# Third layer of a position-bias network on tiles of 32 keys, by a third level of lane sums carried out by DMA

## The chip, the cores and the metric

The kernel runs on one core of a Trainium2 chip. The metric is device time in microseconds (us), lower is better; a time is one execution of the whole program. All data are float32.

## What is computed

Two layers in a row on an input of 2 × 512 × 32 × 32. The first is deformable attention with eight heads followed by a two-layer perceptron; the second is a plain attention over the 1024 positions. The change lies in the first one's position bias, which costs most: for every batch and head (16 groups), every query (1024) and every sampled key (64), a small network 2 → 128 → 128 → 1 is applied to the distance between them.

```python
pos = grid_q[:, :, None, :] - grid_kv[:, None, :, :]
bias = jnp.sign(pos) * jnp.log1p(jnp.abs(pos))
bias = jax.nn.relu(bias @ cpb_w1 + cpb_b1)
bias = jax.nn.relu(bias @ cpb_w2 + cpb_b2)
bias = (bias @ cpb_w3 + cpb_b3).reshape(b, GROUPS, H * W, Hd * Wd)
sim = jnp.einsum('bhid,bhjd->bhij', qh, kh) + bias
attn = jax.nn.softmax(sim, axis=-1)
out = jnp.einsum('bhij,bhjd->bhid', attn, vh)
```

`pos` has two coordinates, so the first layer's value for a query (y, x) and a key is a sum of one table entry for x and one for y, then a relu.

## The kernel before

**The main loop.** There are 16 groups of 16 slots (`NS` = 256 steps in all); a slot is four keys of one group against all 1024 queries. A group is one head of one batch: a block of 128 channels holds two heads. Step s of the loop (L847 on) does the following.

- `st_layer1(s + 2)` (L681): VectorE (DVE) makes the first layer's 128 channels × 4096 values of a slot, two steps ahead, from tables `ta` and `tb`. The tables come from a DMA into `fb` (L650, on SP's queue), once in four steps.
- `st_layer2(s)` (L698): TensorE (PE) multiplies by the second layer's weights. The 128 output channels are taken in four quarters z; each quarter fills a PSUM tile `ps` of two banks in which the four keys lie in four blocks of 32 partitions, and is made of eight float32 matmuls, each of which shows as two instructions. ScalarE (ACT) evicts each quarter with bias and relu: z = 0 and 2 to `rx` (L707), z = 1 and 3 to the sums and to `ub` (L709). There are three `ps` tiles.
- `st_sum(s, z)` (L717): DVE adds two quarters. With z = 2 GpSimd (POOL) then issues an accumulating DMA that adds `ub` to the slot's sum tile (L719).

After that a slot's sum tile holds, for each of four keys, 32 partial sums (lanes) over 1024 queries. The second layer's channels were ordered beforehand (`rank`, `order`, `arrange`), so that the third layer is a sum with signs over lanes.

**The lane sums.** The third layer on PE (`st_layer3`, L784) takes a tile of 128 partitions whatever is in it, so the tiles are first made denser by DMAs from SBUF to SBUF. `st_fold(s)` adds the odd lanes of a tile to the even ones; the odd lanes are free then, and `st_join(s)` puts the next slot's sum in them: a copy on SP's queue (L743) and an accumulating DMA on POOL's (L736). The tile then holds eight keys of 16 lanes. `st_fold2` and `st_join2` do the same once more with pairs of lanes (copy L752), which gives 16 keys of eight lanes. Each of them takes two DMAs[...]. `added[0]` is the newest lane sum; `add` issues each sum behind it on POOL with `tc.issue_after`, which orders issue on one engine and waits for nothing.

**The order in the loop.** A pair of slots that begins at a has its fold in step a + 2 and its join (copy and sum) in step a + 3. Four slots from a have `st_fold2` in step a + 4 and `st_join2` in step a + 6. Every eight slots `st_layer3` runs twelve steps after their first: four matmuls, one for each half of the queries and each of two tiles of 16 keys, in four column blocks of 32. Two such calls fill the group's `sim`, to which the query-key products (`QUADS`, L767) are added. The steps of the softmax (`softmax_steps`) are spread over the following steps behind an eviction. The last slots go to the third layer without the sums (weights `w3u`).

**Buffers.** The sum tiles are `ua` (four buffers, every fourth slot), `uc` (two, every fourth slot), `uo` (three, every second slot); `ub` and `rx` have three each. A sum tile is written by ACT in its own step and is free when its last reader is through: for `uc` and `uo` a join's DMA, for `ua` the third layer.

**Background.** Queries, offsets, sampled keys and values are made in small portions between the steps (`chain`, `sample`), in five chains. `prod` holds 12 tap products of the offset convolution; its borders are cleared once, in `arrange`. After the loop come the output projection (`project`), the perceptron and the second layer.

Of the kernel before, what the change touches and what calls it, by code (L numbers as in the profile page):

```python
# [57 lines left out]
def conv_seq_kernel(ctx: ExitStack, tc: tile.TileContext, x, xt, kst, pst, cst, vec, wsm, outw, w1, w2, wl, wlt, brow, out):  # L58
# [25 lines left out]
    w3f = cp.tile([P, 48], F32, name="w3f")  # L84
# [122 lines left out]
    with tc.tile_pool(name="lp", bufs=2) as lp:  # L207
# [11 lines left out]
        prod = ph.tile([P, 12, 2, 8, 8], F32, name="prod")  # L219
# [22 lines left out]
        nc.gpsimd.dma_start(out=pz[:, 0:413], in_=pst)  # L242
        nc.gpsimd.dma_start(out=ident, in_=kst)

        def load(b, k, wq=None):
# [21 lines left out]
        w2t, crow, tri, eight, chan, mask = (  # L267
            pz[:, a:b] for a, b in ((0, 128), (128, 256), (256, 384), (384, 392), (392, 393), (393, 413))
        )
        wb = vs[:, VOFF["w3"] : VOFF["w3"] + 2]  # L270
        po_, rn, t8, pc, dc, k8, one = (
            pw_[:, a:b] for a, b in ((0, 1), (1, 3), (3, 4), (4, 5), (5, 6), (8, 16), (128, 256))
# [15 lines left out]
        def order():  # L288
            nc.vector.tensor_scalar(k8, eight, rn[:, 1:2], 8.0, ALU.is_le, ALU.mult)
            nc.vector.tensor_reduce(t8, k8, AX.X, ALU.add)  # L290
# [6 lines left out]
        def arrange():  # L297
            nc.gpsimd.memset(prod, 0.0)
# [17 lines left out]
            nc.gpsimd.tensor_scalar(w3f[:, 16:32], mask[:, 0:16], sc[:, 8:9], None, ALU.mult)  # L316
            nc.gpsimd.tensor_scalar(w3u[:, 28:32], mask[:, 16:20], sc[:, 8:9], None, ALU.mult)
# [4 lines left out]
        def chain(ci):  # L322
# [52 lines left out]
            else:  # L375


                for m in range(3):
# [71 lines left out]
            fe = ph.tile([P, 5, n], F32, tag="fe", name="fe")  # L450
            pos, ab, u, ln, er = (fe[0:64, i, :] for i in range(5))
            nc.vector.tensor_scalar(pos, thf[0:64, 2 * n : 3 * n], -1.0, gq[0:64], ALU.mult, ALU.add)
# [8 lines left out]
            nc.vector.scalar_tensor_tensor(er, u, 1.0, ab, ALU.subtract, ALU.subtract)  # L461
            rc = acc.rearrange("p a k y x -> p (a k y x)")[0:64, 0:n]
            nc.vector.reciprocal(rc, u)
            nc.vector.tensor_tensor(er, er, rc, ALU.mult)
            nc.vector.tensor_scalar(pos, pos, 0.0, 2.0, ALU.is_ge, ALU.mult)
            yield
            nc.vector.tensor_tensor(ln, ln, er, ALU.subtract)
# [10 lines left out]
        def sample(ci):  # L478
# [10 lines left out]
            sg = ph.tile([P, 5, 2, K * J], F32, tag="fe", name="sg")  # L489
            hat = sg[:, 0:4].rearrange("p a f j -> p (a f j)")[:, 0 : 4 * K * J]  # L490
# [4 lines left out]
            nc.vector.tensor_tensor(sg[:, 4], sg[:, 0], sg[:, 1], ALU.mult)  # L495
            hx = ph.tile([P, 2, K, J], F32, tag="hx", name="hx")
# [5 lines left out]
            for i, (b, k) in enumerate(G):  # L502
                g = b * NCH + k
                xnt = ph.tile([P, 8, P], F32, name="xnt")
# [12 lines left out]
                kv, uv = (ph.tile([P, J], F32, name=name) for name in ("kv", "uv"))  # L517
                rowwise, natural = "p (e i t) -> p e i t", "p (i e t) -> p e i t"
                for f in range(2):
                    r, v = slice(64 * f, 64 * f + 64), sg[:, 4, f, i * J : (i + 1) * J]  # L520
                    nc.scalar.activation(
                        uv[r].rearrange(rowwise, e=2, t=16), v[r].rearrange(natural, e=2, t=16), AF.Copy,
                        scale=col("bn1b", k)[r],
                    )
# [6 lines left out]
                for t in range(8):  # L531
# [5 lines left out]
                nc.scalar.activation(  # L537
                    kv.rearrange(rowwise, e=2, t=16), ps[:, 0:J].rearrange(natural, e=2, t=16), AF.Copy,
                    scale=bns[:, k : k + 1],
                )  # L540
# [150 lines left out]
        def st_layer2(s):  # L691
            h1 = h1s.pop(s)
            r = []
            for z in range(4):
                ps = zp.tile([P, 2, 512], F32, name="ps2")
                for h in range(2):
# [6 lines left out]
                    ("rx", 3), (("ua", 4), ("uo", 3), ("uc", 2), ("uo", 3))[s % 4], ("rx", 3), ("ub", 3)  # L703
# [34 lines left out]

        def st_fold(s):
            add(lanes(s, 0), lanes(s, 1))  # L740

        def st_join(s):
            nc.sync.dma_start(out=lanes(s, 1), in_=lanes(s + 1, 1))  # L743
            add(lanes(s, 1), lanes(s + 1, 0))
# [4 lines left out]

        def st_join2(s):  # L750
            for o, i in zip(twos(s, 1), twos(s + 2, 1)):
                nc.sync.dma_start(out=o, in_=i)  # L752
            for o, i in zip(twos(s, 1), twos(s + 2, 0)):
                add(o, i)


        def st_layer3(s):
            gi, i = divmod(s // 8, NSL // 8)
            b, k, f = groups[gi]
            if gi not in sims:  # L760
                sims[gi] = simp.tile([P, 512], F32, name="sim")
            if f == 0 and i == 1:

                assert state[chain_of[b, k][0]] is None
                sims[gi + 1] = simp.tile([P, 512], F32, name="sim")
                for f_, h_, o, h in QUADS:
                    nc.tensor.matmul(  # L767
                        sims[gi + o][h_, :], kz[f_, b * NCH + k, :], qa[f_, b, k, h * 512 : (h + 1) * 512],
                        start=(o == 1), stop=False,
                    )  # L770
            w = w3f[:, 16 - 16 * i : 48 - 16 * i]
            parts = [[(w, sums[s + 4 * e][1])] for e in range(2)]
            if s + 8 == NS:

                w = [w3u[:, 28 - 16 * i - 4 * o : 60 - 16 * i - 4 * o] for o in range(4)]
                parts[1] = [(w[o], sums[s + 4 + o][1]) for o in range(4)]
                parts[1].append((w[3], sums[s + 7][3]))
                parts[0] = 4 * [None] + parts[0]
            for m in range(len(parts[1])):
                for h in range(2):  # L780
                    for e in range(2):
                        if parts[e][m]:
                            q, (w_, t) = 64 * h + 32 * e, parts[e][m]
                            nc.tensor.matmul(  # L784
                                sims[gi][q : q + 32, :], w_, t[:, h, :], start=(i == 0 and f == 0),
                                stop=(i == 1 and m == len(parts[e]) - 1),
                            )
# [762 lines left out]
```

## Time and profile before

| What | us |
|---|---|
| median of 3 runs | 2618.96 |
| lowest and highest run | 2618.88, 2620.72 |
| profiled execution, time | 2621.32 |
| profiled execution, span of the core | 2619.2 |
| of it: start of the main loop's matmuls | 37.6 |
| of it: after the loop, from the first matmul of the projection | 1895.6 to 2619.2 |

A busy time is the time in which an engine executes instructions, summed without overlap. PEld is the load of weights into PE, beside the matmuls. In a row of instructions, `out<-in` names the tiles; then come shapes, count, busy time, mean duration in ns, and the idle time of the engine just before these instructions with what ended it.

The DMA queues, their packets, bytes and the share of the 16 DMA engines' time:

```profile
q0 software_dynamic: 100736, 259.43, 54.6%
q1 hardware_dynamic: 66144, 144.93, 15.8%
```

q0 is POOL's queue (the accumulating DMAs), q1 that of SP and ACT.

### The profile page before, as it was taken

The numbers are of one execution on the slowest core, as the hardware profiler recorded it, in microseconds if no ns is written. First come the engines' busy times: TensorE is split into PE (matmuls) and PEld (weight loads), VectorE is DVE, ScalarE is ACT, GpSimd is POOL, SyncE is SP. The second block draws the span as 40 slices with busy tenths as digits, with TensorE's granted clock in tenths as the row PEclk, the third lists the DMA queues.
The fourth block names the chain that finished last, engine by engine and source line by source line (L and its number), as shares of the span: only waits on it lengthen the run. The fifth ranks groups of instructions, "written<-read, shape, count | busy, mean of one in ns | idle before, by whom it ended". The sixth has DMA issues, their size and how long they took to land.

```text
span 2619.2 us, 48156 instructions
## 1 busy us (share of the span) xinstructions
PE 2603.2 (99%) x19752; PEld 1019.5 (39%) x19752; DVE 2313.1 (88%) x1463; ACT 1750.3 (67%) x2325; POOL 815.7 (31%) x909
## 2 busy tenths in 40 slices
PE   9999999999999999999999999999999999999999
PEld 3333322333233232333333333334355665646556
DVE  7999999999999999999999999999776587666656
ACT  5887898878888887887887777777733242314041
POOL 1333333333333333333333333333332334200100
PEclk9999999999999999999999999999999999999999
DMA  5788877888887888787887888788787768400202
GB/s 188 176 174 185 190 171 168 182 182 195 169 178 171 180 171 200 173 179 166 185 182 165 180 177 177 167 185 177 151 211 169 150 143 172 91 17 1 73 0 57
DMA packets 167531, 407.74 MB, mean 156 GB/s; under 512 B 24944, under 2 KB 73216, under 8 KB 164624
## 3 DMA queue, kind: packets, MB, share of 16 engines
q0 software_dynamic: 100736, 259.43, 54.6%
q1 hardware_dynamic: 66144, 144.93, 15.8%
q8 instruction: 156, 2.56, 0.4%
q14 instruction: 63, 0.52, 0.1%
q10 hardware_dynamic: 432, 0.31, 0.0%
HBM read 82.15 MB, written 6.55 MB: 34 GB/s over the span
## 4 chain that ended last, share of the span: by engine, by line
PE 93%; DVE 3%; ACT 2%; issue 1%; DMA 0%; DVEq 0%; ACTq 0%
PE ps L698 64%; PE sw L1041 7%; PE sw L1200 7%; PE sw L160 6%; PE sw L988 2%; PE sw L1298 2%; PE sim L784 1%; PE psg L600 1%; DVE hm L137 1%; ACT rx L707 1%; PE psx L1276 1%; PE pkv L534 0%; PE sim L767 0%; PE pt L801 0%; PE pb L834 0%
## 5 line engine op out<-in xcount | busy, mean ns | idle before, releaser
L698 PE MATMUL ps<-h,cw 128*32 128x512 f32 x16384 | 1776.0, 592 | 6.1 <-ACT rx L707 5.0
L681 DVE CUSTOM_DVE_ANT_1 h<-ta,tb 128x4096 f32<-128x4096 f32 (+1 forms) x257 | 1130.5, 4399 | 29.6 <-PE ps L698 26.8
L698 PEld LDWEIGHTS ps<-h,cw 128*32 128x32 f32 x16384 | 538.0, 110 | 1209.1 <-issue 1144.6
L707 ACT ACTIVATE rx<-ps,sc 128x1024 f32<-128x1024 f32 x512 | 568.2, 1110 | 146.3 <-PE ps L698 125.7
L709 ACT ACTIVATE ub<-ps,sc 128x1024 f32<-128x1024 f32 x256 | 308.3, 1204 | 92.7 <-PE ps L698 92.6
L717 DVE SCALAR_TENSOR_TENSOR ub<-rx,sc,ub 128x1024 f32<-128x1024 f32 x256 | 326.3, 1275 | 6.6 <-ACT ub L709 6.6
L736 POOL DMA_DIRECT2D ua<-uc x126 | 154.8, 1241 | 301.6 <-DMA ua<-uc 291.7
L736 POOL DMA_DIRECT2D ua<-ua x189 | 219.0, 1319 | 28.8 <-DMA ua<-uo 22.3
L719 POOL DMA_DIRECT2D uo<-ub x127 | 124.4, 980 | 232.3 <-DVE ub L717 217.6
L1041 PE MATMUL sw<-hm,w2t 128*128 128x512 f32 x448 | 193.8, 592 | 0.2 <-DVE hm L125 0.2
L709 ACT ACTIVATE uo<-ps,sc 128x1024 f32<-128x1024 f32 x128 | 154.3, 1205 | 51.4 <-PE ps L698 51.0
L717 DVE SCALAR_TENSOR_TENSOR uo<-rx,sc,uo 128x1024 f32<-128x1024 f32 x128 | 163.3, 1276 | 8.1 <-ACT uo L709 8.1
L736 POOL DMA_DIRECT2D uc<-uo x63 | 53.1, 842 | 319.4 <-DMA uc<-uo 314.4
L1041 PEld LDWEIGHTS sw<-hm,w2t 128*128 128x128 f32 x448 | 85.0, 190 | 104.3 <-issue 99.0
L137 DVE TENSOR_TENSOR hm<-hm,sw 128x512 f32<-128x512 f32 (+1 forms) x80 | 58.7, 738 | 70.4 <-PE sw L160 50.6
L719 POOL DMA_DIRECT2D ua<-ub x64 | 58.9, 921 | 170.8 <-DVE ub L717 163.5
L661 ACT ACTIVATE ta<-fb,vs 128x512 f32<-128x512 f32 (+1 forms) x65 | 89.3, 1377 | 8.0 <-DMA fb<-fdr 8.0
L709 ACT ACTIVATE ua<-ps,sc 128x1024 f32<-128x1024 f32 x64 | 77.1, 1204 | 20.4 <-PE ps L698 20.1
L709 ACT ACTIVATE uc<-ps,sc 128x1024 f32<-128x1024 f32 x64 | 77.2, 1206 | 20.2 <-PE ps L698 17.1
L1364 POOL DMA_DIRECT2D xs<-rs x6 | 7.2, 1195 | 259.2 <-DVE rs L137 259.2
L166 ACT COPY hm<-sw 128x512 f32<-128x512 f32 x24 | 14.1, 586 | 110.1 <-PE sw L160 110.1
L717 DVE SCALAR_TENSOR_TENSOR uc<-rx,sc,uc 128x1024 f32<-128x1024 f32 x64 | 81.6, 1275 | 2.7 <-ACT uc L709 2.5
(294 smaller groups left out, 2657.7 us busy)
## 6 DMA issues: line engine op xcount, KB each, us to landing
uo<-ub POOLq DMA_DIRECT2D x127, 512.0 KB, 5.5
fb<-fdr SPq DMA_DIRECT2D x64, 512.0 KB, 5.2
ua<-ub POOLq DMA_DIRECT2D x64, 512.0 KB, 5.7
uc<-ub POOLq DMA_DIRECT2D x64, 512.0 KB, 5.1
ua<-ua POOLq DMA_DIRECT2D x63, 256.0 KB, 6.2
ua<-uo SPq DMA_DIRECT2D x63, 256.0 KB, 2.4
ua<-uo POOLq DMA_DIRECT2D x63, 256.0 KB, 5.8
uc<-uc POOLq DMA_DIRECT2D x63, 256.0 KB, 6.9
```

What stands on the lines that cost most here:

```text
L137: nc.vector.tensor_tensor(out, a, b_, op)
L160: nc.tensor.matmul(bank[:, e, :], w, x, start=(q in (1, 2, 5) and e == k == 0), stop=True, skip_group_check=True,)
L661: nc.scalar.activation(ta.rearrange("p j x -> p x j")[:, :, j0:j1], fb[:, 0, :, j0:j1], AF.Identity, bias=col("cb1"), scale=col("w1x"),)
L681: nc.vector._custom_dve(TENSOR_ADD_SAT, out=h1[:, y : y + step].rearrange("p y t x -> p (y t x)"), in0=a.unsqueeze(1).to_broadcast([P, ste ...
L698: nc.tensor.matmul(ps[32 * q : 32 * q + 32, h, :], cw2[:, 32 * z : 32 * z + 32], h1[:, 16 * h : 16 * h + 16, q, :], start=True, stop=True,)
L707: nc.scalar.activation(o, ps, AF.Relu, bias=sc[:, 4 + z : 5 + z])
L709: nc.scalar.activation(o, ps, AF.Relu, bias=sc[:, 4 + z : 5 + z], scale=sc[:, z : z + 1])
L717: nc.vector.scalar_tensor_tensor(r[1], r[0], sc[:, z : z + 1], r[1], ALU.mult, ALU.add)
L719: nc.gpsimd.dma_start(out=sums[s][1], in_=sums[s][3], accum_op=ALU.add)
L736: nc.gpsimd.dma_start(out=out, in_=in_, accum_op=ALU.add)
L1041: nc.tensor.matmul(ps[:, m, :], w[:, a, k, m * P : (m + 1) * P], x[:, b_, k, :], start=(k == 0), stop=(k == 1),)
L1200: nc.tensor.matmul(ps[:, m, :], w[:, a, k, c + m * P : c + (m + 1) * P], x[b_][:, k, :], start=(k == 0), stop=(k == nk - 1),)
```

## The change

**A third level of lane sums.** `fours`, `st_fold3`, `st_copy3` and `st_join3` treat eight slots as the second level treats four: partitions of a tile are taken as 16 blocks of two times four, and each of fold, copy and join takes four DMAs of 16 partitions × 1024 elements (64 KB). A tile then holds 32 keys of four lanes. This is done for slots below `FULL` (208), which are groups 0 to 12; groups 13 to 15 stay with 16 keys to a tile.

**The third layer.** `st_layer3` takes a whole group: in groups 0 to 12 four matmuls on two tiles, in groups 13 and 14 eight on four tiles, in group 15 sixteen at the end as before, of which four stood in a call of their own. The query-key products open both of the `sim` tiles of a pair. The call stands 27 steps after the group's first slot (22 in groups 13 and 14), and the softmax steps are queued from there. Before, the second call of a group stood 20 steps after its first slot.

**The order.** A table `LEVELS` names the steps: fold, copy and join of the first level 2, 3 and 4 steps after a pair's first slot, of the second 6, 7 and 8 steps after, of the third 11, 14 and 15. The joins' copies are now moves of their own one step ahead of the sums, issued through `move`, which puts the SP copy into `tc.issue_after(added[0])`. In the last group times are near those of before (`LAST`).

**Buffers.** `ua` becomes `u8` (four buffers, every eighth slot) and `u4` (two, every eighth slot, four slots later). To make room `prod` shares the gather's buffer `xnt` and is cleared on POOL in each of chains 1 to 4, `fe` and `sg` shrink from five parts to three by working in place, `hx` shares `acc`, `kv` and `uv` share `gof`, and `opt` is allocated after the loop. The keys stay in natural order, so `uv` and `kv` are plain copies.

**Constants.** `order` needs one comparison in place of a comparison and a sum; the weight masks `w3f` are wider.

```diff
-                    ("rx", 3), (("ua", 4), ("uo", 3), ("uc", 2), ("uo", 3))[s % 4], ("rx", 3), ("ub", 3)
+                    ("rx", 3), (("u8", 4), ("uo", 3), ("uc", 2), ("uo", 3), ("u4", 2), ("uo", 3), ("uc", 2), ("uo", 3))[s % 8],
+                    ("rx", 3), ("ub", 3),
...
+        def move(out, in_):
+            with tc.issue_after(added[0]):
+                nc.sync.dma_start(out=out, in_=in_)
+
         def st_fold(s):
             add(lanes(s, 0), lanes(s, 1))
 
+        def st_copy(s):
+            move(lanes(s, 1), lanes(s + 1, 1))
+
         def st_join(s):
-            nc.sync.dma_start(out=lanes(s, 1), in_=lanes(s + 1, 1))
             add(lanes(s, 1), lanes(s + 1, 0))
...
+        def st_copy2(s):
+            for o, i in zip(twos(s, 1), twos(s + 2, 1)):
+                move(o, i)
+
         def st_join2(s):
-            for o, i in zip(twos(s, 1), twos(s + 2, 1)):
-                nc.sync.dma_start(out=o, in_=i)
             for o, i in zip(twos(s, 1), twos(s + 2, 0)):
                 add(o, i)
 
+        def fours(s, i):
+            t = sums[s][1].rearrange("(l a e) h n -> l a e (h n)", a=2, e=4)[:, i]
+            return [t[:, e] for e in range(4)]
+
+        def st_fold3(s):
+            for o, i in zip(fours(s, 0), fours(s, 1)):
+                add(o, i)
+
+        def st_copy3(s):
+            for o, i in zip(fours(s, 1), fours(s + 4, 1)):
+                move(o, i)
+
+        def st_join3(s):
+            for o, i in zip(fours(s, 1), fours(s + 4, 0)):
+                add(o, i)
+
+        FULL = NS - 3 * NSL
+        LEVELS = (
+            (8, FULL, (st_copy3, st_join3, st_fold3), (14, 15, 11)),
+            (4, NS - 4, (st_copy2, st_join2, st_fold2), (7, 8, 6)),
+            (2, NS - 4, (st_copy, st_join, st_fold), (3, 4, 2)),
+        )
+        LAST = {st_copy2: 6, st_join2: 6, st_fold2: 4, st_join: 3}
+        due = {}
+        for step, end, moves, times in LEVELS:
+            for kind in range(3):
+                for a in range(0, end, step):
+                    t = times[kind] if a < NS - NSL else LAST.get(moves[kind], times[kind])
+                    due.setdefault(a + t, []).append((kind > 0, moves[kind], a))
...
         def st_layer3(s):
-            gi, i = divmod(s // 8, NSL // 8)
+            gi = s // NSL
...
-            w = w3f[:, 16 - 16 * i : 48 - 16 * i]
-            parts = [[(w, sums[s + 4 * e][1])] for e in range(2)]
-            if s + 8 == NS:
...
+            if s < FULL:
+                parts = [[(w3f[:, 0:32], sums[s + 8 * i][1])] for i in range(2)]
+            else:
+                w = [w3f[:, 48 - 16 * e : 80 - 16 * e] for e in range(2)]
+                parts = [[(w[e], sums[s + 8 * i + 4 * e][1]) for e in range(2)] for i in range(2)]
+            if s + NSL == NS:
...
-            if s % 2 == 0 and 2 <= s < NS - 2:
-                st_fold(s - 2)
-            if s % 2 == 1 and 3 <= s < NS - 1:
-                st_join(s - 3)
-            if s % 4 == 0 and s >= 4:
-                st_fold2(s - 4)
-            if s % 4 == 2 and s >= 6:
-                st_join2(s - 6)
+            for _, go, a in sorted(due.get(s, ()), key=lambda e: e[0]):
+                go(a)
...
-            if s % 8 == 4 and s >= 12:
-                st_layer3(s - 12)
-                if s % NSL == 4:
-                    tails.append(softmax_steps(s // NSL - 1))
+            for t in (27, 22):
+                if s % NSL == t % NSL and s >= t and (s - t < FULL) == (t == 27):
+                    st_layer3(s - t)
+                    tails.append(softmax_steps((s - t) // NSL))
         st_sum(NS - 1, 2)
-        st_layer3(NS - 8)
+        st_layer3(NS - NSL)
```

In the chains (`chain`, `sample`):

```diff
-            nc.gpsimd.memset(prod, 0.0)
...
+                prod = ph.tile([P, 12, 2, 8, 8], F32, tag="xnt", name="prod")
+                nc.gpsimd.memset(prod, 0.0)
...
-            hx = ph.tile([P, 2, K, J], F32, tag="hx", name="hx")
+            hx = ph.tile([P, 2, K, J], F32, tag="acc", name="hx")
...
-                kv, uv = (ph.tile([P, J], F32, name=name) for name in ("kv", "uv"))
+                both = ph.tile([P, 2, J], F32, tag="gof", name="both")
+                kv, uv = both[:, 0], both[:, 1]
```

## The prediction

> **What bounds the kernel now.** I read the busy times, then three stretches of the execution, then TensorE's costliest groups with what ended their idle time, then timelines. First the busy times, and the main loop alone (37.6 to 1895.6 us; columns: length, then busy us and instructions of PE, PEld, DVE, ACT, POOL, granted clock, DMA share, GB/s):
>
> ```profile
> PE 2603.2 (99%) x19752; PEld 1019.5 (39%) x19752; DVE 2313.1 (88%) x1463; ACT 1750.3 (67%) x2325; POOL 815.7 (31%) x909
> ```
>
> ```profile
> 37.60:1895.60 1858.00, 1851.81 (x17304) 578.03 (x17303) 1808.14 (x909) 1519.38 (x1978) 651.66 (x760) 1.00 0.82 176
> ```
>
> PE idles 6.2 us in 1858. The loop is TensorE's, at full clock, and work taken from PE there comes off the end, provided nothing new starves it. Two neighbours are close: DVE is 97.3% busy there, the DMA engines 82%.
>
> ```profile
> L698 PE MATMUL ps<-h,cw 128*32 128x512 f32 x16384 | 1776.0, 592 | 6.1 <-ACT rx L707 5.0
> L784 PE MATMUL sim<-ua,w3f 128*32 128x512 f32 x252 | 35.0, 596 | 0.0
> ```
>
> The first row is layer 2 (64 instructions a step, 256 steps), the second the third layer, which the change halves. Neither shows waits worth naming. What one third-layer call costs PE stands in its timeline:
>
> ```profile
> 1411.78 4.04 PE L698 MATMUL ps<-h,cw 128*32 128x512 f32 x36
> 1415.64 1.04 PE L784 MATMUL sim<-ua,w3f 128*32 128x512 f32 x8
> 1416.50 13.92 PE L698 MATMUL ps<-h,cw 128*32 128x512 f32 x128
> ```
>
> The busy span of a call is 1.04 us, but it overlaps its neighbours: it starts at 1415.64 and layer 2 goes on at 1416.50, so it moves everything behind it by 0.86 us.
>
> **Two places of the Trainium skill.** "TensorE: Matmul & The Clock Gate", Part 3 (packing small matmuls), says that matmuls on different column tiles run at once and take about one matmul's duration plus a few ns each. The trace agrees: eight instructions of 592 ns, four column tiles twice, cost 0.86 us and not 4.7. I go by the 0.86. "SBUF — State Buffer", Door 1 (the DMA port swizzle), derives the port from partition bits 4 to 2 and bit 6. The present pieces step over 2 or 4 partitions and reach all 16 ports; the new ones (`fours`) step over 8 and reach half. No row of before shows such a step, so this enters as an upper bound below.
>
> **Part by part, against the profiled span of 2619.2 us** (2621.3 us with what lies around it; the timed runs' median is 2618.96, so I carry differences over to the median).
>
> Third layer. Before, 31 full calls of four matmuls (eight instructions) and a last call of twelve matmuls. After, groups 0 to 12 need one call of four matmuls instead of two; groups 13 to 15 keep their number. 13 calls of 0.86 us: **−11.2 us**, all on PE's path. The bound is 13 × 1.04 = 13.5, if nothing overlapped. The 64 query-key matmuls (L767) stay, only their start flag and place change: 0.
>
> New lane sums. Eight steps issue 24 accumulating DMAs on POOL now (8 of L719, 16 of L736) and will issue 32. POOL starts queued ones 0.53 to 0.57 us apart (1459.99, 1460.56, 1461.09 below), so +4.4 us in some 58; POOL is busy 35% of the loop. What it loses now is blocking: joins wait for the copy issued in their own step.
>
> ```profile
> POOL uc L736 <- DMA uc<-uo: 314.4, 61, 9.4
> POOL ua L736 <- DMA ua<-uc: 291.7, 55, 7.7
> ```
>
> (total us, times, longest.) With each copy a step ahead of its join, most of these 606 us of blocking should go. That is no gain in itself, as nobody on PE's path waits for POOL now, but it pays for the eight extra issues. Value: 0.
>
> Traffic. Eight steps move by software 4 MB of L719 plus 3 MB of folds and joins; the third level adds 8 × 64 KB, 7%. By the SP queue they move 1 MB of tables and 1.5 MB of copies; it adds 256 KB, 10%. From 600 to 1800 us the two queues hold 67.9% and 13.9% of the engines' time, so 0.82 becomes about 0.88; at half the ports and twice the price per byte, 0.94. DMA has no direct path to PE; it acts through buffers, next.
>
> Buffers. `uc` is the tight one: two buffers, one taken every fourth step, so a tile is written again eight steps later. Its last reader, `st_join2`, moves from four steps after the tile's own step to six. ACT writes one tile and its successor here:
>
> ```profile
> 1427.05 1.21 ACT L709 ACTIVATE uc<-ps,sc 128x1024 f32<-128x1024 f32 x1 [0.60 <-PE ps L698]
> ...
> 1483.56 1.20 ACT L709 ACTIVATE uc<-ps,sc 128x1024 f32<-128x1024 f32 x1 [0.60 <-PE ps L698]
> ```
>
> and POOL, around its reader:
>
> ```profile
> 1459.99 0.88 POOL L719 DMA_DIRECT2D uo<-ub  x1 [3.34 <-DVE ub L717]
> 1460.56 1.17 POOL L736 DMA_DIRECT2D ua<-ua  x1
> 1461.09 1.49 POOL L736 DMA_DIRECT2D ua<-uc  x1
> 1465.61 0.81 POOL L736 DMA_DIRECT2D ua<-uc  x1 [3.03 <-DMA ua<-uc]
> 1466.72 0.88 POOL L719 DMA_DIRECT2D uc<-ub  x1 [0.30 <-DVE ub L717]
> 1469.38 0.84 POOL L736 DMA_DIRECT2D ua<-uo  x1 [1.79 <-DMA ua<-uo]
> 1473.44 0.88 POOL L719 DMA_DIRECT2D uo<-ub  x1 [3.22 <-DVE ub L717]
> ```
>
> Now the last read is issued at 1465.61 and lands about 1471: 12 us to spare. After, it stands in the step that opens at 1473.44, second behind that sum: 1474.5. That leaves 9.0 us to 1483.56. The same reckoning over 60 such tiles gives 5.6 to 13.1 us, median 9.9. The folds and joins take
>
> ```profile
> DMA to landing us min/median/max: 2.5/5.8/9.4
> ```
>
> (L736, 600 to 1800 us). A typical tile is free some 4 us early. If landings grow by 1 to 2 us with the load, about one tile in six is late by 1 to 2 us. Behind a late `uc` eviction stand all of ACT's later evictions; PE can fill two more of three PSUM pairs, 2 × 1.72 us less the 1.2 us eviction, so 2.2 us are absorbed. Value: **+1.5 us**; bounds 0 and 50 (52 tiles by 1 us). The other buffers have more room: `uo` is read one step later of six; `u4` has 5 of 16 steps left after its last step, `u8` 5 of 32.
>
> SP. Copies and table loads share its queue. A table lands in about 5 us and is used some 26 us after its issue (SP issues one at 1415.46, ACT reads it at 1442.61), so a blocked SP costs nothing below 20 us.
>
> DVE. 1808 us must fit in 1847: 97.9%. From 1200 to 1500 us it is busy 298.2 of 300 while the change asks for 2.2 us less; the two steps that layer 1 runs ahead cover this: 0, at worst +0.5.
>
> `prod` now lives in the gather's buffer and is cleared on POOL in each of four chains (1.4 us each; ACT's tap multiplies behind it would wait). The buffer's last reader is several steps earlier, so the clearing can go ahead: +0.3, bound +6 (four times one POOL burst). Reused small tiles (`fe`, `acc`, `gof`), contiguous `uv` and `kv` copies and the vector operation gone from `order` are off the path: before 37.6 us PE runs L600 back to back.
>
> End. The softmax tail of group 14 starts two steps later, so two exponential pairs (4 × 0.53 us) land behind the loop, under 3.9 us in which ACT waits for PE's last sums: 0. Should other work fill that gap, +2. `opt` only gets another place.
>
> Sum: −11.2 + 1.5 + 0.3 = −9.4, so 2618.96 − 9.4 ≈ **2609.5 us**.
>
> **Rivals.**
> (a) Given back: late `uc` tiles, the clearing and the tail together cost 6 to 16 us; 2614 to 2624, no change to speak of. For it: DMA at 82% before anything is added. Against: only 2.4 us of ACT waiting on `uc` now.
> (b) Slower: `uc` becomes the bound. From a mean landing that uses up the 9.9 us of room and the 2.2 us of PSUM, every further 0.1 us costs 52 × 0.1 = 5.2 us; it decides from a mean excess of 0.2 us. At 0.5 us: 2619 − 11 + 26 = 2634. For it: the half-port pieces, chains of fold, copy, join one step apart with 6 us landings in 7.2 us steps, and an L736 maximum of 9.4 us. Against: POOL is no longer blocked, and a stalled PE gives back room at once.
> (c) The hold on copies does nothing: `move` asks for order behind a sum on POOL, but the copy is issued by SP, and the code's other uses order only what shares the engine. Copies then go when ready, as now; a badly placed one delays a join by some us. About 2612.
>
> **How the numbers follow.** Forecast 0.55 (own range 2606 to 2613), (c) 0.05, (a) 0.15, (b) 0.25. Differences under 0.2% (5.2 us) can't be told from none here. Faster: 0.55 + 0.05 = 0.60; same 0.15; slower 0.25. The range runs from 2605.5 (13.5 us saved) to 2632 (half of (b)).
>
> **What would show it.** L784 down from 252 `w3f` instructions to about 148, loop PE idle still under 10 us, POOL's waits for copies mostly gone, DMA share 0.86 to 0.90, landings up by no more than 1 us. I am wrong if ACT's `uc` evictions wait for a DMA by tens of us, if PE's idle time in the loop grows by as much as 11 us, or if layer 1 on DVE starts to end PE's waits.

## The result: slower, and the profile after

| | before | after |
|---|---|---|
| median, us (4 runs each) | 2619.59 | 2638.93 |
| lowest and highest run | 2618.88, 2620.72 | 2638.08, 2641.51 |
| ratio, 95% interval | | 1.0075 [1.0058, 1.0093] |
| profiled execution, span | 2619.2 | 2636.3 |
| start of the last layer-2 matmul | 1891.6 | 1893.5 |
| start of the last softmax transposes (`pb`) | 1911.1 | 1926.6 |

The change costs 19 us where 9 us were to be gained. The table already says where to look: the main loop ends 1.9 us later than before, and 13.6 us more are lost between the loop and the transposes. (The other 1.6 us of the span's 17.1 come later, mostly at the first perceptron weights, for which PE waits 1.4 us; before, it didn't wait there. The profiled execution of before took 2621.32 us, 1.7 above the median, so differences of spans come out smaller than those of medians.)

The page of after, in the parts that answer to those shown of before (busy times, DMA queues, TensorE's costliest row):

```profile
PE 2598.5 (99%) x19648; PEld 1003.7 (38%) x19648; DVE 2309.7 (88%) x1462; ACT 1746.7 (66%) x2324; POOL 980.0 (37%) x1121
...
q0 software_dynamic: 107392, 273.09, 58.1%
q1 hardware_dynamic: 69472, 151.75, 17.1%
...
L693 PE MATMUL ps<-h,cw 128*32 128x512 f32 x16384 | 1776.8, 593 | 15.2 <-ACT rx L703 10.0
```

Layer 2 is L693 now. PE's work has shrunk by 104 instructions, but the idle time ahead of layer 2 has grown from 6.1 to 15.2 us.

What PE waited for in the loop and just after it, from the groups of after between 37 and 1912 us (idle us before the instructions, then its releasers):

```profile
L819 PE MATMUL sim<-u,w3f 128*32 128x512 f32 x148 | 22.4, 612 | 11.0 <-DMA u<-uc 11.0
```

The third layer has 148 `w3f` instructions instead of 252, as forecast. It also has one wait of 11.0 us that no call had before. PE's timeline around it, first of before, then of after (start us, duration, and in brackets the idle time before it):

```profile
1892.05 1.03 PE L784 MATMUL sim<-ua,w3u 128*32 128x512 f32 x4
1892.91 1.03 PE L784 MATMUL sim<-uo,w3u 128*32 128x512 f32 x4
```

```profile
1893.98 1.12 PE L1016 MATMUL sw<-qa,vp 128*128 128x512 f32 x2
1906.15 1.92 PE L819 MATMUL sim<-u,w3f 128*32 128x512 f32 x4 [11.04 <-DMA u<-uc]
1907.83 1.95 PE L819 MATMUL sim<-u,w3u 128*32 128x512 f32 x4
```

Before, the last group's third layer follows layer 2 at once. After, it waits for the last second-level join to land (`u<-uc`, slot 248), and four instructions (two matmuls) then take 1.92 us instead of 1.03. The 1.92 is the clock, as the stretches of after show (length, busy us and instructions of PE, PEld, DVE, ACT, POOL, granted clock, DMA share, GB/s):

```profile
1894.00:1906.00 12.00, 1.11 (x6) 0.28 (x2) 1.28 (x1) 2.56 (x8) 3.38 (x4) 0.73 0.59 131
1906.00:1910.00 4.00, 3.85 (x11) 1.09 (x14) 0.00 (x0) 0.00 (x0) 0.00 (x0) 0.53 0.02 4
1910.00:1914.00 4.00, 4.00 (x26) 1.31 (x21) 0.67 (x1) 0.67 (x1) 0.61 (x1) 1.00 0.00 0
```

The granted clock sinks during the wait and stays at 0.53 for the first 4 us of work. The first eight instructions take 3.4 us, not 1.7. So 11.0 (wait) + 1.7 (clock) + 0.9 (the four matmuls whose call stood inside the loop before) make the 13.6 us.

Why was the join late? POOL's timeline of before and of after:

```profile
1888.27 0.81 POOL L736 DMA_DIRECT2D ua<-uc  x1 [5.17 <-DMA ua<-uc]
```

```profile
1845.02 0.83 POOL L732 DMA_DIRECT2D u<-uc  x1 [10.82 <-DMA u<-uc]
...
1885.25 0.82 POOL L732 DMA_DIRECT2D u<-u  x1 [2.64 <-DMA u<-uo]
1885.78 1.17 POOL L732 DMA_DIRECT2D uc<-uc  x1
...
1895.88 0.83 POOL L732 DMA_DIRECT2D uc<-uo  x1 [7.16 <-DMA u<-uc]
...
1903.40 0.81 POOL L732 DMA_DIRECT2D u<-uc  x1 [4.95 <-DMA u<-uc]
```

The last join is issued at 1903.40 instead of 1888.27. Two things lie ahead of it in POOL's queue, where the sums keep the order that `added[0]` gives them: each of these waits holds all that stand behind it. Inside the last group a second-level sum (`u<-u` at 1885.25, which waits for a join to land) now stands ahead of the first-level fold `uc<-uc`, so the copy and the join behind that fold come late too (the 7.16 us at 1895.88). And earlier, at 1845.02, the queue already stood 10.82 us. It stood for a copy that waited for the join `uc<-uo`, which POOL had issued at 1832.39, just behind slot 244's own sum (`u<-ub` at 1831.85). That slot's tile is a `u4`, and ACT wrote it late:

```profile
1826.09 1.20 ACT L705 ACTIVATE ub<-ps,sc 128x1024 f32<-128x1024 f32 x1 [0.28 <-PE ps L693]
1828.94 1.21 ACT L705 ACTIVATE u<-ps,sc 128x1024 f32<-128x1024 f32 x1 [1.65 <-PE sim L819]
```

An eviction should wait for `ps`, the matmul that fills its PSUM pair. This one waits for `sim`, the third-layer call of group 14, which reads the old content of its buffer. It comes two slots after its turn: ACT has evicted slot 246's `uc` (1822.65) before it.

### The profile page after: what moved, and what is told of

Its sections match the earlier page's. It is cut to its first block, busy times and chain, and to the rows that moved or that the text cites. A ratio compares the mean times of both kernels' runs of the same rounds, so it can differ in the third digit from the quotient of the medians.

```text
span 2636.3 us, 48908 instructions
## 1 busy us (share of the span) xinstructions
PE 2598.5 (99%) x19648; PEld 1003.7 (38%) x19648; DVE 2309.7 (88%) x1462; ACT 1746.7 (66%) x2324; POOL 980.0 (37%) x1121
## 3 DMA queue, kind: packets, MB, share of 16 engines
q1 hardware_dynamic: 69472, 151.75, 17.1%
## 4 chain that ended last, share of the span: by engine, by line
PE 62%; DVE 11%; issue 10%; DMA 10%; POOL 4%; ACT 2%; SPq 0%; DVEq 0%; POOLq 0%; ACTq 0%
PE ps L693 37%; PE sw L1069 7%; PE sw L1230 7%; PE sw L160 6%; DVE h L676 4%; DMA u<-uc 3%; DMA uc<-uc 3%; POOL u L732 2%; DVE ub L713 2%; PE sw L1328 2%; DMA uc<-uo 1%; PE psg L595 1%; DMA u<-u 1%; DVE uo L713 1%; DVE hm L137 1%
## 5 line engine op out<-in xcount | busy, mean ns | idle before, releaser
L693 PE MATMUL ps<-h,cw 128*32 128x512 f32 x16384 | 1776.8, 593 | 15.2 <-ACT rx L703 10.0
L693 PEld LDWEIGHTS ps<-h,cw 128*32 128x32 f32 x16384 | 525.6, 110 | 1235.5 <-issue 1137.7
L732 POOL DMA_DIRECT2D u<-u x397 | 403.1, 1484 | 17.0 <-DMA u<-ub 6.4
L713 DVE SCALAR_TENSOR_TENSOR ub<-rx,sc,ub 128x1024 f32<-128x1024 f32 x256 | 327.0, 1277 | 10.5 <-ACT ub L705 10.5
L715 POOL DMA_DIRECT2D uo<-ub x127 | 114.0, 898 | 584.9 <-DVE ub L713 537.4
L732 POOL DMA_DIRECT2D u<-uc x126 | 125.4, 1268 | 33.0 <-DMA u<-uc 31.5
L715 POOL DMA_DIRECT2D uc<-ub x64 | 57.2, 894 | 188.8 <-DVE ub L713 147.9
L715 POOL DMA_DIRECT2D u<-ub x64 | 56.5, 882 | 173.2 <-DVE ub L713 171.6
L732 POOL DMA_DIRECT2D uc<-uc x63 | 109.1, 1732 | 0.0
L732 POOL DMA_DIRECT2D uc<-uo x63 | 94.0, 1492 | 27.4 <-DMA u<-uc 13.3
L732 POOL DMA_DIRECT2D u<-uo x63 | 87.9, 1396 | 20.9 <-DMA u<-uo 17.0
```

The lines of the kernel that those rows point to most:

```text
L693: nc.tensor.matmul(ps[32 * q : 32 * q + 32, h, :], cw2[:, 32 * z : 32 * z + 32], h1[:, 16 * h : 16 * h + 16, q, :], start=True, stop=True,)
L713: nc.vector.scalar_tensor_tensor(r[1], r[0], sc[:, z : z + 1], r[1], ALU.mult, ALU.add)
L715: nc.gpsimd.dma_start(out=sums[s][1], in_=sums[s][3], accum_op=ALU.add)
L732: nc.gpsimd.dma_start(out=out, in_=in_, accum_op=ALU.add)
```

## The experiments

For PE's stalls I took, from the trace of each kernel, the time by which each quarter of a layer-2 step (16 instructions, 1.72 us) without other matmuls exceeds that pace, up to the loop's end; work at a lowered clock counts in it. "End" is the change of the span, "loop" that of the last layer-2 matmul, both against the profile of before. Each ratio is against runs of before taken beside that kernel (their medians lie between 2619.3 and 2619.8).

| kernel | median us | ratio, 95% | PE stalls | loop | wait ahead of last call | end |
|---|---|---|---|---|---|---|
| before | 2619.6 | | 9.0 | | none | |
| after | 2638.9 | 1.0075 [1.0058, 1.0093] | 21.0 | +1.9 | 11.0 | +17.1 |
| 1: another buffer for slot 228 | 2627.7 | 1.0030 [1.0020, 1.0041] | 15.4 | −2.2 | 5.4 | +8.3 |
| 2: old order in the last group | 2625.7 | 1.0026 [1.0015, 1.0037] | 19.1 | +0.1 | 2.0 | +4.7 |
| 3: 1, and tile 248 read last | 2630.0 | 1.0041 [1.0026, 1.0056] | 14.1 | −3.0 | 6.3 | +8.5 |
| 4: no third level | 2633.7 | 1.0054 [1.0039, 1.0069] | 9.6 | +2.1 | 7.9 | +12.8 |
| 5: 1 and 2 | 2620.9 | 1.0004 [0.9996, 1.0012] | 13.9 | −3.5 | none | −0.2 |
| 6: 5, second level a step earlier | 2640.6 | 1.0083 [1.0069, 1.0096] | 29.1 | +15.1 | none | +16.8 |
| 7: 5, steps of before | 2725.8 | 1.0408 [1.0394, 1.0422] | 121.3 | +106.4 | none | +109.7 |
| 8: 2 and 4 | 2623.9 | 1.0019 [1.0012, 1.0025] | 9.5 | +1.9 | none | +2.5 |
| 9: 5, old order in every step | 2631.4 | 1.0044 [1.0030, 1.0058] | 24.2 | +6.2 | none | +10.4 |
| 10: 5, first weights earlier | 2619.0 | 0.9997 [0.9988, 1.0005] | 15.2 | −2.2 | none | −0.4 |
| 11: before, first weights earlier | 2620.2 | 1.0003 [0.9995, 1.0011] | 7.2 | −0.7 | none | −0.3 |

The columns from one profile each carry chance: runs 10 and 11 leave the loops of run 5 and of before as they are, and yet differ from them by 1.3 and 0.7 us in "loop" and by 1.3 and 1.8 us in stalls.

**1. A buffer for slot 228.** Theory A: the shortage of `u4` starts in group 13. Its slot 212 is read by the third-layer call 18 steps later, but its buffer is due after 16, at slot 228. The same holds for slot 228, in group 14, and slot 244. With slot 228 in a `u8`, slot 244 takes the buffer of slot 220, which is read in time.

```diff
-("rx", 3), (("u8", 4), ("uo", 3), ("uc", 2), ("uo", 3), ("u4", 2), ("uo", 3), ("uc", 2), ("uo", 3))[s % 8],
+("rx", 3), (("u8", 4), ("uo", 3), ("uc", 2), ("uo", 3), ("u4", 2), ("uo", 3), ("uc", 2), ("uo", 3))[0 if s == 228 else s % 8],
```

> The changed kernel with the sum tile of slot 228 taken from u8 instead of u4, nothing else. Theory A (u4 has two buffers and a tile of groups 13 and 14 is held until their third-layer call 22 steps after the group's first slot, so slots 228 and 244 can't evict their second quarter for two to three steps, slot 244's sum is late, all lane sums queued behind it are late, and PE meets the unfinished tile of slot 248 at the end): the 11.0 us wait at the third layer's end shrinks below 4 us, PE's stalls in steps 226 to 255 fall from 5.6 us to under 1.5, time 2619 to 2625 us. Theory B (the last group's lane sums are late by their own order on POOL, whatever the buffers): the wait stays above 8 us and the time above 2633 us.

The stalls after 1300 us are gone (0.3 us, against 5.8 in after) and 11.2 us of the time with them. The last join is issued at 1892.72. 5.4 us of the wait at the end stay, more than the 4 that I had set. A holds, but for part of it.

**2. The old order in the last group.** Theory B: the sort by kind (folds and joins together) and level lets a second-level sum pass a first-level one within a step.

```diff
-                    due.setdefault(a + t, []).append((kind > 0, moves[kind], a))
+                    k = kind > 0 if a < NS - NSL else (kind > 0) + (1 if step == 2 else 3)
+                    due.setdefault(a + t, []).append((k, moves[kind], a))
```

> The changed kernel with the last group's lane sums in the order of the kernel before (first level ahead of the second in a step), u4 left as it is. Theory B (order on POOL): the wait for slot 248's tile falls below 4 us, time 2619 to 2627 us. Theory A (u4 buffers): slot 244's eviction is as late as in the changed kernel, the wait at the end stays above 6 us, time 2631 us or more.

The wait at the end falls to 2.0 us though the `u4` stalls remain. B holds in part too. Each repair hides some of what the other would bring: −11.2 and −13.2 us alone, −18.0 together (run 5).

**3. Tile 248 read last.** In after, the tile of slot 248 stands first in PE's last call; before, it stood behind the single tiles.

```diff
-                parts[1][1:] = [(w[o], sums[s + 12 + o][1]) for o in range(4)] + [(w[3], sums[s + 15][3])]
+                parts[1] = [(w[o], sums[s + 12 + o][1]) for o in range(4)] + [(w[3], sums[s + 15][3])] + parts[1][:1]
```

> As the first run (slot 228 from u8), and in the last call of the third layer the matmuls on the tile of slot 248 stand last in their column blocks, as in the kernel before, and no longer first. If PE's queue order adds to the wait at the end once the sums are in time, this is 1 to 5 us below the first run; if the tile is ready before PE arrives, the two agree within 1 us.

A miss: it is not below run 1. PE's longest wait in this kernel (us in total, times, longest):

```profile
PE sim L819 <- DMA uc<-ub: 5.8, 1, 5.8
```

The call starts earlier and then stops at slot 254, whose own sum is queued on POOL behind the same join. The order on POOL must be mended, not the one on PE.

**4. No third level.**

```diff
-        FULL = NS - 3 * NSL
+        FULL = 0
...
-                    ("rx", 3), (("u8", 4), ("uo", 3), ("uc", 2), ("uo", 3), ("u4", 2), ("uo", 3), ("uc", 2), ("uo", 3))[s % 8],
+                    ("rx", 3), (("ua", 6), ("uo", 3), ("uc", 2), ("uo", 3))[s % 4],
```

> The changed kernel without its third level of lane sums: all groups as its groups 13 and 14, sum tiles of every fourth slot from one set of six buffers. PE does 13 x 0.86 = 11.2 us more than in the changed kernel, traffic and POOL issues are those of the kernel before, the steps of the first two levels those of the changed kernel. If the third level's traffic causes the loop's new stalls outside the last groups (14.5 us of pure PE stall from 300 to 1300 us against 8 before), they fall to 10 or less and the time is 2619 to 2623 us. If the later joins and copies or the shared small buffers cause them, they stay at 13 or more and the time is 2624 to 2632 us.

The time missed what I expected, because I had not counted the wait at the end as a cost of the order by itself. The loop did what it should: stalls at 9.6 us, as before. So the added stalls elsewhere in the loop belong to the third level, while 7.9 us of waiting appear without it and without any shortage of `u4` (the row names no releaser; run 8 shows that the order is behind it):

```profile
L819 PE MATMUL sim<-ua,w3f 128*32 128x512 f32 x252 | 35.0, 605 | 7.9 <-issue 7.9
```

**5. Both repairs.**

> The changed kernel with both repairs: slot 228's sum tile from u8, and the last group's lane sums in the order of the kernel before. If the wait at the end has these two causes and no third, PE waits less than 1.5 us there, the projection after the loop starts no more than 1 us later than in the kernel before, and the time is 2616 to 2621 us; what is left of the 11.2 us of PE work saved is eaten by the loop's stalls (15 us against 9). If a third cause sits in the end, the wait stays above 3 us and the time above 2623 us.

As expected: the slowdown is gone, and the last join is issued at 1884.85. The loop ends 3.5 us earlier than before, yet the span only gains 0.2. PE's timeline shows where it goes, at the first perceptron matmul:

```profile
1955.01 1.13 PE L160 MATMUL sw<-xb,w1e 128*128 128x256 f32 x4 [2.17 <-DMA w1e<-w1e]
```

It waits for the perceptron's weight sums, a chain of transfers on POOL whose last is issued at 1942.31 us here and at 1942.52 in before.

**6 and 7. The steps.** Run 6 puts the second level one step earlier, `(6, 7, 5)` in place of `(7, 8, 6)`. Run 7 goes back to the steps of before, copy and join in one step and the second level earlier, and to the old order in every step. The edit of run 7, against after:

```diff
-            (4, NS - 4, (st_copy2, st_join2, st_fold2), (7, 8, 6)),
-            (2, NS - 4, (st_copy, st_join, st_fold), (3, 4, 2)),
+            (4, NS - 4, (st_copy2, st_join2, st_fold2), (6, 6, 4)),
+            (2, NS - 4, (st_copy, st_join, st_fold), (3, 3, 2)),
...
-                    due.setdefault(a + t, []).append((kind > 0, moves[kind], a))
+                    k = (kind > 0) + {2: 1, 4: 3, 8: 5}[step]
+                    due.setdefault(a + t, []).append((k, moves[kind], a))
```

> As the run before, with fold, copy and join of the second level one step earlier (5, 6, 7 steps after the first slot instead of 6, 7, 8), so that a uc tile is free one step sooner. If late uc tiles cost PE its stall near 900 us (2.9 us), ACT's waits of uc evictions for DMAs (12 us in the first of these repairs) fall below 3 us and the time falls by 2 to 4 us against the run before. If uc does not matter, nothing changes beyond 1 us; if the earlier fold blocks POOL, the time rises.

> As the first of these three, with the first two levels everywhere at the steps and in the order of the kernel before (copy and join in one step, second level at 4 and 6), and the third level as changed. If the new steps themselves cost the loop its stalls (bursts on POOL, later joins), pure PE stall falls from 15 to 10 us or less and the time to 2611 to 2616 us. If the third level's traffic costs them, stall stays at 13 or more and the time within 2 us of the first run; if POOL's blocking on copies now hurts, with 8 more issues in eight steps, the time rises above 2622 us.

Run 6 is a miss. POOL's waits in it:

```profile
POOL uc L732 <- DMA u<-uc: 427.4, 60, 11.3
POOL u L732 <- DMA u<-uo: 342.9, 108, 8.1
```

The first row is the first-level join into `uc`, which waits for the second level's copy out of it. With (6, 7, 5) this copy falls into the step of the join that should come first, and copies are issued first in a step. So the edit does more than I said: the copy takes lanes to which the join has not yet added its part, and the kernel of run 6 leaves out a quarter of the lanes of every fourth slot's sum. Its time shows what such waits cost, 770 us of POOL and 15 us of the loop, and not what an earlier second level would be worth. The second row is mostly the second level's fold, which now comes one step (7.2 us) after the join that it needs, while a landing takes up to 10.5.

In run 7 POOL stands for copies as it did before the change (541.8 us in joins to `uc` and 355.9 in those to `u`, against 314.4 and 291.7), and now that hurts. The waits of ACT and of PE there:

```profile
ACT ub L705 <- DMA uc<-ub: 107.2, 32, 6.7
```

```profile
PE ps L693 <- ACT ub L705: 61.1, 32, 4.1
```

Sums of `ub` are queued behind blocked joins, and `ub` has three buffers. With a third level on the queue, steps and order that were free in before cost some 105 us. The old order by itself costs 10.5 of them with the new steps (run 9), which leaves some 94 us for the steps. Whether the joint copies or the earlier second level cost more, run 7 doesn't separate.

**8. No third level, and the old order in the last group.**

> No third level in any group (each group's third layer in four calls' worth of matmuls, sum tiles as in the kernel before), and the last group's sums in the order of the kernel before. My theory: without the third level the loop has neither its saving of PE work (about 11 us) nor its added PE stalls (stalls beyond the pace of layer 2 again at 9 to 10 us), and with the old order the wait of 7.9 us at the end goes: 2618 to 2622 us, the last layer-2 matmul within 1.5 us of the kernel before, no wait over 2 us ahead of the last third-layer call. Then what the third level is worth is read from the loop's end of this kernel against that of the kernel with both repairs (about 3 us, not 11). Rival: the step between copies and adds in the first two levels itself costs or gains something; then the loop's end moves by more than 2 us against the kernel before.

The stalls are as expected, and the wait at the end is gone, so the order alone costs 9.7 us here (run 4 against run 8). The loop ends 1.9 us late where at most 1.5 was expected, and the time is 2 us above the band. This is the bill of the change without its third level: +4.6 us against before (ratio 1.0019 [1.0012, 1.0025]). Against run 5 it prices the third level by itself: the loop ends 5.4 us earlier with it while the stalls are 4.4 us longer, so by this reckoning some 9.8 us of PE work are saved and not quite half is lost to stalls.

Nearly all of the 4.4 us is one stall. In run 5 ACT waits for a load of `xn`, an input of the background work, and PE for ACT (ACT's waits, then PE's timeline):

```profile
ACT xn L328 <- DMA xn<-in_x: 5.3, 1, 5.3
```

```profile
321.71 3.20 PE L693 MATMUL ps<-h,cw 128*32 128x512 f32 x16 [3.68 <-ACT rx L703]
```

This stall is 3.9 us of run 5's 13.9; in run 8 it is absent, and in after and runs 1, 2, 3 and 10 it is 2.7 to 3.8. The load lands 11.1 us after its issue in run 5, 7.0 in run 8 and 8.9 in before, where ACT starts on it as it lands. No run moved this load, so it isn't shown that an earlier issue would bring the 3.9 us back.

**9. The old order in every step.**

```diff
-                    due.setdefault(a + t, []).append((kind > 0, moves[kind], a))
+                    k = (kind > 0) + {2: 1, 4: 3, 8: 5}[step]
+                    due.setdefault(a + t, []).append((k, moves[kind], a))
```

> Both repairs, and in every step of the loop the first level's sums ahead of the second's, and those ahead of the third's; the steps stay those of the changed kernel. My theory: the order within a step matters only where PE waits for the last sums, so within 2 us of the kernel with both repairs (2618 to 2623 us), PE's stalls in the loop at 12 to 16 us. Rival: in the loop too, a second-level sum that is queued ahead of a first-level one passes its wait on to the next slot's tiles, and part of the loop's 5 us of added stalls comes from that: stalls at 11 us or less and 2614 to 2618 us. Other rival: a first-level join put ahead waits for its copy, which was issued one step before, and holds the third level's sums back: over 2624 us.

My expectation fell. The time is on the last rival's side, but joins that wait for copies are little of it: POOL's largest such wait grew from 23.6 us in run 5 to 44.5. The mechanism is one of the prediction. ACT's waits:

```profile
ACT uc L705 <- DMA u<-uc: 56.4, 29, 5.1
```

`u<-uc` is the second-level join, the last reader of `uc`. With a first-level sum put ahead of it, 29 of the 64 `uc` tiles come late; in after one does, by 3.4 us (two others by less than 1). The same order that costs 7 us in the last group saves 10 us in the loop.

**10 and 11. The weights after the loop.** The first perceptron weights are issued after four pieces of x instead of eight, in run 5's kernel and, as a control, in before.

```diff
-            if i == 1:
+            if i == 0:
                 load_first(0)
                 load_inner(0)
```

> Both repairs, and the first unit's perceptron weights (the load of w1x, its sums on POOL's queue and the copies and sums of w1e) issued after the first four pieces of x instead of after eight, so some 1.8 us earlier on SP. My theory: with both repairs the end of the loop is 3 us earlier than before, and this is lost where PE waits 2.2 us for the last sum of w1e, which comes at the end of a chain of transfers. Then an earlier start of that chain brings the gain back: the first perceptron matmul 1 to 2 us ahead of the one of the kernel with both repairs, 2616.5 to 2619 us. Rival: the chain is set by the rate of all transfers in this stretch (20 pieces of x and of weights share it), not by its start: the last sum of w1e comes when it did, or x's last pieces come later, 2619.5 to 2622 us.

> The kernel before with the same edit as the other kernel of this call, as a control. My theory: in the kernel before PE comes to the first perceptron matmul no earlier than the sums of w1e, so an earlier chain brings nothing: 2618.5 to 2620.5 us. If it gains as much as the other, the edit is worth its time by itself and says nothing of the third level.

The first sum of the chain starts 1.3 us earlier than in run 5, and the last comes when it did. POOL's timeline of run 10:

```profile
1908.09 1.76 POOL L972 DMA_DIRECT2D w1x<-w1x  x2 [5.59 <-DMA w1x<-in_w]
...
1942.46 1.43 POOL L972 DMA_DIRECT2D w1e<-w1e  x1 [4.62 <-DMA w1e<-w1e]
```

So the chain's start doesn't set its end, and neither run can be told from before. What does set it stays open; in run 5 17 MB pass in the 90 us around it, and the later links took longer in run 10.

No kernel tried is faster than before by what can be measured.

## Why the prediction was wrong

**Two steps failed, and with them "End … 0".** The first is the sentence "`u4` has 5 of 16 steps left after its last step". It is true of groups 0 to 12, where the third-level join reads the tile 11 steps after its slot. In groups 13 and 14 there is no such join; the third-layer call is the last reader, 18 steps after the slot, and the buffer comes round after 16. I counted readers in the new part of the change and not in the groups that it leaves out. Mended alone, this is worth 11.2 us (run 1).

The second is **the last group's order**, which I put at nothing without examining it: its times were near the old ones, and I took the order within a step for the old one too. Mended alone it is worth 13.2 us (run 2), with the first failing removed 6.8 us (run 1 against run 5). Both make the last join late, and PE waits 11.0 us for it at the end, at a place where the forecast had no wait.

Then the terms of the sum.

- Third layer, −11.2: right in kind, some 9.8 us by runs 5 and 8, which is within the chance of those columns.
- Buffers, `uc`, +1.5: the right kind, and luck in the size. Only one tile came more than 1 us late, where I had reckoned with one in six, but it cost 4.2 us: ACT waits 3.4 us, PE 2.35, so 1.1 us were absorbed and not 2.2, and PE then works 3.4 us at half its clock (last section). Rival (b) named the true danger, as run 9 shows, but not for this order.
- DVE, 0 and at worst +0.5: too small. ACT's waits for `ub` on DVE went from 13.9 to 50.4 us, and 11.4 in run 8. DVE is busy 1032.2 of 1050 us in mid-loop, against 1028.1. What this costs PE wasn't isolated; beside the stall for `xn`, some 0.5 of the 4.4 us of stalls in run 5 against 8 are left for it.
- DMA with "no direct path to PE", acting through buffers: there was a short path that I hadn't listed, the load of `xn` that ACT reads between evictions. At 316 us of after PE stalls 2.7 us because ACT waits 4.1 us for it (10.2 us to land instead of 8.9). Without the third level (runs 4 and 8) this stall is absent.
- Traffic. The middle of the loop, before and after:

```profile
600.00:1650.00 1050.00, 1047.22 (x9786) 322.37 (x9782) 1028.10 (x513) 860.43 (x1130) 374.54 (x437) 1.00 0.83 178
```

```profile
600.00:1650.00 1050.00, 1045.56 (x9746) 317.82 (x9742) 1032.16 (x515) 859.18 (x1124) 486.65 (x579) 1.00 0.92 192
```

  A share of 0.92 against 0.86 to 0.90 forecast, inside my bounds. In this stretch POOL's queue moved 7.2% more bytes (133.5 to 143.2 MB) and took 10.5% more engine time (67.8 to 74.9%), so the added bytes cost about 1.45 times the others, an estimate that lays all the added time to them. Whether it is their ports or the fuller engines that cost this, no run separates. The Trainium skill's "SBUF — State Buffer", Door 1, from whose ports I took the factor of two as an upper bound, agrees with it in sign.
- POOL's waits for copies, "mostly gone": right. Of 314 and 292 us these are left:

```profile
POOL u L732 <- DMA u<-uc: 31.5, 7, 10.8
...
POOL uc L732 <- DMA uc<-uo: 13.1, 10, 3.2
```

  That it "pays for the eight extra issues" was more than right: with the steps and the order of before, the kernel with them takes some 105 us more (run 7).
- Rival (c), the hold that does nothing: true of the program. Without the hold it has the same instructions in the same order on every engine.

The whole, in medians: +4.6 for the change without its third level (run 8), −3.0 for the third level (run 5 against 8), +18.0 for the two faults at the end (after against run 5). These three add up to the change by construction (19.6, against 19.3 from the first runs), so the sum is a bill and no test. Of the 28.7 us between −9.4 and +19.3, the faults at the end are 18.0. The 4.6 us had, but for the 0.3 of `prod`, no place in the forecast and stay open: the copies' new steps and the shared small buffers weren't separated, and of the 1.9 us by which run 8's loop ends late, PE's stalls explain 0.5.

## What to carry to other kernels

When a change treats most groups in a new way and leaves some in the old, reckon each buffer's last reader for both kinds: the shortage is in the remainder. Where sums pass through a queue that issues in order, the best order in the steady loop (free the scarcest buffer first) can be the worst one in the last group (shortest chain to the end first). And work saved on the busiest engine is kept only while everything it needs comes in time: here one load that used to land just as it was read took 3.9 of some 9.8 us.

## What the runs showed of the hardware

A wait of TensorE can cost 1.7 us more than its length. The late `uc` tile in after, a wait of 2.35 us (timeline of PE, then stretches of 1 us with the columns of above):

```profile
902.95 7.41 PE L693 MATMUL ps<-h,cw 128*32 128x512 f32 x52 [2.35 <-ACT uc L705]
```

```profile
901.00:902.00 1.00, 0.00 (x0) 0.00 (x0) 1.00 (x1) 0.31 (x1) 0.00 (x0) 1.00 1.10 217
902.00:903.00 1.00, 0.05 (x4) 0.06 (x8) 1.00 (x2) 1.00 (x2) 0.00 (x0) 0.93 1.01 201
903.00:904.00 1.00, 1.00 (x8) 0.34 (x12) 1.00 (x2) 1.00 (x5) 0.00 (x0) 0.50 0.97 221
904.00:905.00 1.00, 1.00 (x12) 0.20 (x4) 1.00 (x2) 1.00 (x2) 0.94 (x2) 0.50 0.34 90
905.00:906.00 1.00, 1.00 (x8) 0.20 (x4) 1.00 (x1) 1.00 (x3) 1.00 (x2) 0.50 0.69 254
906.00:907.00 1.00, 1.00 (x12) 0.24 (x8) 1.00 (x1) 1.00 (x4) 0.60 (x1) 0.86 1.05 209
```

The clock falls as PE begins again and stays at half for 3.4 us, a loss of 1.7. Another wait of after, of 2.52 us at 318, was followed by a full clock; in run 5 the wait there was 3.68 us and the clock fell. In before it is full all through the loop. In the thirteen traces, none of 41 waits of PE from 1.1 to 1.95 us was followed by the half clock, nine of 23 from 1.98 to 3.51 us were, and all 15 from 3.53 us up. So 1.7 us of a difference between two of these kernels can be chance. The Trainium skill's "TensorE: Matmul & The Clock Gate", Part 1, has the clock fall after an idle window of about 3.4 us and come back after as much work. The second agrees (3.4 us here, 3.7 after the wait of 11 us at the end). The first doesn't hold as a bound on a single wait: 1.98 us (run 6) were enough once, and 3.51 us (run 7) were not. So a stall had a step in its price here: up to 1.95 us it cost its length, up to 3.5 us sometimes as much as 1.7 us more, and beyond that always something more.

The lane sums' landings (L732 of after, 600 to 1650 us) were 2.5/5.8/9.4 us in before and

```profile
DMA to landing us min/median/max: 4.2/6.7/10.5
```

now. I had put such growth down to traffic beforehand, and nearly all of it is not: run 8, with a share of 0.82 and no third level, has 4.7/6.6/10.1. What these two share, against before, is the copies' own step. Their sums leave POOL in bunches instead of one by one behind their copies, which may be why; no run tests it.
